# A three-layer graph network: another form of the last layer's sums, and gathers moved ahead of a layer's last rows

## The chip, the cores and the metric

The kernel runs on one core of a Trainium2 chip. The metric is device time in microseconds (us), lower is better. One launch computes the whole result; all inputs come from HBM and the output goes back there. A core has TensorE (PE in the profile; PEld is its weight load), VectorE (DVE), ScalarE (ACT), GpSimd (POOL) and SyncE (SP); each runs its own list of instructions in order, and waits on semaphores for the others. Indirect DMAs, which fetch or store rows whose numbers lie in a tile of indices, are issued by GpSimd. SP issues the plain ones.

## The reference

A graph of N = 6250 nodes and 100,000 edges (`src`, `dst`, sorted by `dst`), with 256 features for each node in float32. Three attention layers follow each other; the first two (GATv2, 4 heads of 64) also have an edge from each node to itself:

```python
xl = (x @ Wl).reshape(n, H, C); xr = (x @ Wr).reshape(n, H, C)
e = leaky_relu(xl[src] + xr[dst], 0.2)
logits = einsum('ehc,hc->eh', e, att)
alpha = softmax of logits over the edges that share a dst
out = segment_sum(xl[src] * alpha[:, :, None], dst) + b
...
x = layernorm(x + gat2(elu(gat1(x))))
...
Wh = einsum('nf,hfd->hnd', x, W)                        # 8 heads of 32
e = leaky_relu(s1[:, src] + s2[:, dst], 0.2)            # s1, s2: Wh times two vectors
out = segment_sum(softmax of e * Wh[:, src], dst)
x = layernorm(x + out)
```

So each layer fetches one row of a table for each edge, weighs it, and adds up the rows of each node.

## The kernel before

**The plan.** `make_plan` first sorts the nodes by falling degree into 49 blocks of 128 nodes, one node on each partition. Block b has a fixed number of columns `cols[b]`, the most edges that a node of it may have: 38, 25, 24, 23, 22, 21, 21, 20, ... down to 10, 10, 9, together 814. Column j of a block holds the j-th source of each of its 128 nodes; nodes with fewer edges point at a row `NP` that adds nothing. The plan leaves, for each block, the sources' numbers and the input rows (`near_d`), and writes the first table `xl1_d`, whose 261st element is the node's place in the sorted order. A flag `fits` says whether the degrees fit the columns; if not, `tile_general_path` computes everything in another way. With `fits` set, `tile_by_degree` runs.

**The three layers of `tile_by_degree`.** `layer2` runs twice (i = 0 and 1), then comes the third layer as a loop of its own. Each walks over the 49 blocks in order, and writes the next layer's table as it goes: layer 1 the rows of `xl2_d` and `xr2_d`, layer 2 those of `wh_d` (in the profile `whs_d`), layer 3 the output. Since any node can be a source, a layer's gathers read the whole table before them. The order is written out by hand, and the engines follow it.

For each column of a block `gather` issues one indirect DMA (128 rows of 260 to 264 floats) into row tiles of up to T = 9 columns; `chunks` cuts a block of up to 9, 18, 27 columns into 1, 2, 3 tiles, block 0 into 5. Layers 1 and 2 have 7 row tiles each, in pools of their own, layer 3 has 8. Block b + 1 is gathered ahead of the work on block b; how far GpSimd runs ahead is set by free row tiles.

In layers 1 and 2 VectorE computes, tile by tile, the maximum `z` (L1331, with weights prepared so that it gives the leaky ReLU), its product with `at` (L1332) and the sum over each head (L1333), in one of three `z` tiles. Then come the largest logit `top` (L1198), ScalarE's exponentials and their sums (L1205), the reciprocal (L1377), and the weighing of the rows (`weighted_sum`, L1235 on VectorE and L1234 on ScalarE); TensorE adds the rows up by multiplying each with the identity into `acc` (L1242). `end` of the block before and `finish` make the next table's row and send it with SP (L1430, L1431, L1463). At the start of layer 2 SP loads blocks 0 to 2 of both tables into `two` (L1439, L1440), later block b + 3.

In layer 3 TensorE does nothing. VectorE adds up the logits (L1496, L1500), finds the maximum (L1198), and after the exponentials weighs the rows in place (L1253). Then `added_up` sums the columns by halves: the second and third row tile are added to the first (L1262), then its upper half to its lower until two columns are left (L1265), and those two give `acc_v` (L1269). The rest is the normalisation (L1507, L1510, L1276, L1278, L1285) and an indirect DMA that scatters the block's rows to the output (`put_out`, L1525). The scatter of block b - 2 stands on GpSimd's queue behind the gathers of block b + 1.

After layer 1, `sources` (the numbers by which layer 1 gathers) are not needed; ScalarE has copied each row's 261st element into `spots` (L1343), by which layers 2 and 3 gather.

## Time and profile before

| | us |
|---|---|
| device time, median of 3 runs | 3926.89 |
| lowest and highest run | 3918.14, 3933.62 |
| device time of the profiled execution | 3945.85 |
| its span, first to last instruction | 3944.1 |
| first gather of layer 1, 2, 3 | 161.8, 1471.1, 2708.2 |
| last gather of layer 3 | 3905.5 |

The profiled execution is one of the longer ones: it lies 19 us above the median of the three runs. In the profile a group of instructions is named by its line, engine, operation and tiles, with its count, its busy time, the mean duration, and the time for which the engine stood idle just before it with what ended that. The mean granted clock of TensorE is 0.67 of full speed. The timeline has start, duration, engine, line and operation, and in brackets the idle time before it with its releaser ("issue" where nothing is seen that it waited for, "remote" where the releaser isn't known).

### The profile page before, as it was taken

The page shows a single profiled execution, that of the slowest core. Times are in us where ns is not written, and L with a number is a line of the kernel's source. Part 1 is how long each engine was busy: PE and PEld are TensorE (multiplying, and loading weights), DVE is VectorE, ACT ScalarE, POOL GpSimd, SP SyncE. Part 2 cuts the span into 40 slices and gives each one's busy share as a digit, 9 for nine tenths or more (in the row PEclk, how much of TensorE's full clock was granted, in tenths as well). Part 3 has the DMA queues.
Part 4 walks back from the last instruction along what each step waited for, and adds up shares of the span by engine and source line. Part 5 has one row for each costly group of instructions (what it writes and reads, how often), then busy time and mean ns, then how long its engine had stood idle before and what let it go on. Part 6 is the DMA issues. An engine that isn't in the chain of part 4 may idle for free.

```text
span 3944.1 us, 23710 instructions
## 1 busy us (share of the span) xinstructions
PE 1485.0 (38%) x5144; PEld 1107.1 (28%) x5145; DVE 2724.0 (69%) x2731; ACT 1102.9 (28%) x4179; POOL 2582.6 (65%) x2640
## 2 busy tenths in 40 slices
PE   5336556556676761455545455552000000000000
PEld 4224434344554541343433343442000000000000
DVE  6277778678788876888877888983655545444554
ACT  2124334334444441343434343541000000000000
POOL 6466666666666636666666666654777777776675
PEclk7667778777788886777666767776555555555555
DMA  8443333333343424343333343433333333333332
GB/s 185 103 96 99 98 100 105 100 98 102 104 107 103 106 74 101 98 111 107 106 107 107 106 112 104 118 104 58 102 100 97 102 99 100 99 97 84 82 99 72
DMA packets 197564, 399.63 MB, mean 101 GB/s; under 512 B 63516, under 2 KB 115994, under 8 KB 197396
## 3 DMA queue, kind: packets, MB, share of 16 engines
q0 software_dynamic: 123488, 342.06, 33.6%
q1 hardware_dynamic: 66226, 54.22, 4.8%
q10 hardware_dynamic: 7698, 1.74, 0.4%
q8 instruction: 45, 0.74, 0.1%
q14 instruction: 107, 0.88, 0.1%
HBM read 357.84 MB, written 40.42 MB: 101 GB/s over the span
## 4 chain that ended last, share of the span: by engine, by line
issue 23%; POOL 22%; DVE 15%; PE 13%; another core or an unknown queue 9%; ACT 6%; DMA 2%; DVEq 0%; ACTq 0%; POOLq 0%
POOL g L1485 15%; PE acc L1242 9%; POOL g L1311 5%; DVE z L1332 4%; DVE z L1331 4%; PE pm L1187 3%; ACT g L1234 3%; DVE lg L1333 2%; ACT wt L1205 2%; DVE g L1235 1%; DVE g L1253 1%; POOL out L1525 1%; ACT xT L1182 1%; DMA g<-whs_d,spots 1%
## 5 line engine op out<-in xcount | busy, mean ns | idle before, releaser
L1242 PE MATMUL acc<-g,ident 128*128 128x256 f32 x3452 | 1038.7, 462 | 940.8 <-issue 368.9
L1242 PEld LDWEIGHTS acc<-g,ident 128*128 128x128 f32 x3452 | 778.1, 233 | 1197.6 <-issue 618.4
L1311 POOL DMA_INDIRECT g<-xl_d,spots x814 | 772.5, 949 | 465.2 <-issue 227.5
L1311 POOL DMA_INDIRECT g<-xl_d,near_r x814 | 774.8, 952 | 427.8 <-issue 239.2
L1485 POOL DMA_INDIRECT g<-whs_d,spots x814 | 857.3, 1053 | 299.0 <-issue 292.6
L1234 ACT ACTIVATE g<-g,by 128x64 f32<-128x64 f32 x2064 | 560.2, 337 | 431.4 <-issue 429.4
L1331 DVE TENSOR_TENSOR z<-g,pr 128x1820 f32<-128x1820 f32 (+4 forms) x236 | 502.3, 2129 | 60.9 <-DMA g<-xl_d,spots 31.9
L1332 DVE TENSOR_TENSOR z<-z,at 128x1820 f32<-128x1820 f32 (+4 forms) x236 | 503.8, 2135 | 8.1
L1333 DVE TENSOR_REDUCE lg<-z 128x28 f32<-128x1820 f32 (+4 forms) x236 | 503.6, 2134 | 8.2
L1235 DVE TENSOR_TENSOR g<-g,wt 128x1792 f32<-128x1792 f32 (+5 forms) x236 | 354.0, 1518 | 2.9
L1215 ACT ACTIVATE wt<-lg 128x128 f32<-128x128 f32 (+17 forms) x49 | 14.0, 285 | 849.3 <-DVE lg L1214 245.2
L1496 DVE TENSOR_TENSOR lg<-g,s_r 128x56 f32<-128x56 f32 (+4 forms) x113 | 25.1, 223 | 314.3 <-DMA g<-whs_d,spots 281.8
L1253 DVE TENSOR_TENSOR g<-g,wt 128x1792 f32<-128x1792 f32 (+4 forms) x113 | 229.5, 2049 | 0.0
L1182 ACT COPY xT<-pt 128x256 f32<-128x256 f32 x147 | 55.0, 374 | 581.9 <-PE pt L1180 341.8
L1377 DVE RECIPROCAL den<-den 128x4 f32<-128x4 f32 x98 | 17.4, 178 | 240.6 <-ACT wt L1205 186.3
L1205 ACT ACTIVATE wt<-lg,top 128x19 f32<-128x19 f32 (+14 forms) x392 | 116.1, 296 | 219.9 <-DVE lg L1333 129.1
L1348 DVE TENSOR_TENSOR h<-acc,den 128x256 f32<-128x256 f32 x98 | 40.9, 417 | 158.6 <-remote 91.6
L1187 PE MATMUL pm<-wcat,xT 128*128 128x260 f32 x392 | 136.2, 506 | 35.9 <-ACT xT L1182 34.5
L1262 DVE TENSOR_TENSOR g<-g,g 128x1792 f32<-128x1792 f32 (+4 forms) x64 | 129.1, 2017 | 25.2 <-DVE g L1253 15.7
L1187 PE MATMUL pm<-wh_cat,xT 128*128 128x272 f32 x196 | 83.2, 564 | 128.9 <-ACT xT L1182 80.3
L1187 PEld LDWEIGHTS pm<-wcat,xT 128*128 128x128 f32 x392 | 95.5, 257 | 71.5 <-ACT xT L1182 50.9
L1525 POOL DMA_INDIRECT out<-y,node_i x49 | 51.4, 1049 | 70.0 <-ACT y L1288 54.4
(162 smaller groups left out, 1575.5 us busy)
## 6 DMA issues: line engine op xcount, KB each, us to landing
g<-xl_d,near_r POOLq DMA_INDIRECT x814
g<-xl_d,spots POOLq DMA_INDIRECT x814
g<-whs_d,spots POOLq DMA_INDIRECT x814
whs_d<-row SPq DMA_DIRECT2D x49, 132.0 KB
xl_d<-xl SPq DMA_DIRECT2D x49, 130.0 KB
xl_d<-row SPq DMA_DIRECT2D x49, 130.0 KB
xr_d<-row SPq DMA_DIRECT2D x49, 130.0 KB
two<-xl_d SPq DMA_DIRECT2D x49, 130.0 KB
```

The lines of the kernel that those rows point to most:

```text
L1187: nc.tensor.matmul(pm, xT[:, c, :], w[:, c, :], start=c == 0, stop=c == 1)
L1205: nc.scalar.activation(wt[:, :, h], lg[:, :S, h], AF.Exp, bias=top[:, h : h + 1], accum_out=den[:, h : h + 1],)
L1234: nc.scalar.mul(g4[:, t, h, :], g4[:, t, h, :], by[:, t - m, h : h + 1])
L1235: nc.vector.tensor_mul(g4[:, :m], g4[:, :m], wt[:, s0 : s0 + m, :].unsqueeze(3).to_broadcast([P, m, H, F // H]),)
L1242: nc.tensor.matmul(acc, ident, g4[:, t], start=s0 + t == 0, stop=s0 + t == S - 1)
L1253: nc.vector.tensor_mul(g4, g4, wt[:, s0:s1, :].unsqueeze(3).to_broadcast([P, n, H, width]))
L1262: nc.vector.tensor_add(t[:, :m], t[:, :m], u[:, :m])
L1311: nc.gpsimd.indirect_dma_start(out=g[:, s - s0, :], out_offset=None, in_=table, in_offset=source(of, b, s - 1),)
L1331: nc.vector.tensor_max(z, g[:, :n, :W2], xr[:, None, :].to_broadcast([P, n, W2]))
L1332: nc.vector.tensor_mul(z, z, at[:, None, :].to_broadcast([P, n, W2]))
L1333: nc.vector.reduce_sum(lg[:, s0:s1, :], z.rearrange("p t (h d) -> p t h d", h=H2), axis=AX.X)
L1485: nc.gpsimd.indirect_dma_start(out=g[:, s - s0, :], out_offset=None, in_=wh_d[:, :], in_offset=source(spots, b, s),)
```

## The change

It has four parts.

1. *Sums of layer 3.* The weighed rows go into a tile of their own, `prod` (up to 27 columns), in place of the row tile. One reduction then sums its columns, reading with a stride of 256 floats. Block 0, with 38 columns, takes two reductions and an addition.
2. *Gathers ahead of the last rows.* The sources of blocks 0, 1 and 2 are sorted by place during layer 1, by keys (place, column) with MAX8 and MATCH_REPLACE8, eight at a time. Of block 0 the first 14, of block 1 the first 12 and of block 2 the first 11 columns then name rows of blocks 0 to 44 alone, copied into `soon`. They are gathered from that part of the table before the last four blocks' rows are there: the calls stand behind the gathers of block 48 of the layer before, for layer 2 and for layer 3. SP's loads of `two` for blocks 0 to 2 move there too.
3. *Row tiles.* One pool of nine serves all three layers, with rows of 264 floats. To make room there is one `z` tile in place of three, `spots` lies in the memory of `sources`, and layer 3 has two `lg` tiles in place of three.
4. *A flag.* If any of the 37 columns names a later row, `done` stays 0. It is read at the end, and `tile_general_path` then computes everything; it is no longer the other branch of `fits`.

```diff
+EARLY = (14, 12, 11)
+LATE = 4
...
-    with tc.If(ok != 0) as branch:
+    with tc.If(ok != 0):
...
-    with branch.Else():
+    right = nc.values_load(done[0:1, 0:1], min_val=0, max_val=1)
+    with tc.If(right == 0):
         tile_general_path(
...
-    spots = consts.tile([P, NB, CM], I32, name="spots")
+    spots = sources
+    AHEAD = (NB - LATE) * P
+    KEY = CM.bit_length()
+    CK = -(-CM // 8) * 8
...
+    rowp = ctx.enter_context(tc.tile_pool(name="rows", bufs=9))
+    twop = ctx.enter_context(tc.tile_pool(name="two", bufs=3))
+    RW = max(W2 + 1, A1)
+    begun = {}
...
+    def gather_rows(b, rows, cut, own, table, of, width, j0, j1):
+        for g, (s0, s1) in zip(rows, cut):
+            for j in range(max(s0 - own, j0), min(s1 - own, j1)):
+                nc.gpsimd.indirect_dma_start(
+                    out=g[:, j + own - s0, :width], out_offset=None, in_=table,
+                    in_offset=source(of, b, j),
+                )
+
+    def row_tiles(b, own):
+        cut = chunks(cols[b] + own)
+        return [rowp.tile([P, T, RW], F32, name="g") for _ in cut], cut
+
+    def begin(own, table, width):
+        for b, n in enumerate(EARLY):
+            begun[b] = row_tiles(b, own)
+            gather_rows(b, *begun[b], own, table[:AHEAD], soon, width, 0, n)
+
+    def sort_sources(work, ps, b):
+        n = cols[b]
+        keys = work.tile([P, CK], F32, name="keys")
+        nc.vector.memset(keys, -float(NP << KEY))
+        nc.vector.tensor_single_scalar(
+            keys[:, :n], spots[:, b, :n], -float(1 << KEY), op=OP.mult
+        )
+        nc.vector.tensor_sub(keys, keys, number)
+        order = work.tile([P, CK], F32, name="order")
+        for r in range(0, CK, 8):
+            nc.vector.max(order[:, r : r + 8], keys)
+            if r + 8 < CK:
+                nc.vector.match_replace(keys, order[:, r : r + 8], keys, -BIG)
+        places = work.tile([P, CK], I32, name="places")
+        nc.vector.tensor_single_scalar(places, order, -1.0, op=OP.mult)
+        nc.vector.tensor_single_scalar(spots[:, b, :n], places[:, :n], KEY, op=OP.logical_shift_right)
+        e = EARLY[b]
+        nc.vector.tensor_single_scalar(soon[:, b, :e], spots[:, b, :e], AHEAD - 1, op=OP.min)
+        nc.vector.tensor_single_scalar(
+            late[:, b : b + 1], spots[:, b, e - 1 : e], float(AHEAD), op=OP.is_ge
+        )
+        if b + 1 == len(EARLY):
+            pb = ps.tile([P, b + 1], F32, name="pb", tag="tp")
+            nc.tensor.matmul(pb, ones, late, start=True, stop=True)
+            bad = work.tile([P, 1], F32, name="bad")
+            nc.vector.reduce_sum(bad, pb, axis=AX.X)
+            nc.vector.tensor_single_scalar(done, bad, 0.0, op=OP.is_equal)
...
-    def added_up(work, rows, cut, wts, H, width, between):
+    def added_up(work, prod, rows, cut, wts, H, width, between):
         wt, _ = wts
-        parts = []
-        for g, (s0, s1) in zip(rows, cut):
+        acc = work.tile([P, F], F32, name="acc_v", bufs=2)
+        base = 0
+        for k, (g, (s0, s1)) in enumerate(zip(rows, cut)):
             n = s1 - s0
-            g4 = g[:, :n, : H * width].rearrange("p t (h d) -> p t h d", h=H)
             nc.vector.tensor_mul(
-                g4, g4, wt[:, s0:s1, :].unsqueeze(3).to_broadcast([P, n, H, width])
+                prod[:, s0 - base : s1 - base, :].rearrange("p t (h d) -> p t h d", h=H),
+                g[:, :n, :F].rearrange("p t (h d) -> p t h d", h=H),
+                wt[:, s0:s1, :].unsqueeze(3).to_broadcast([P, n, H, width]),
             )
             if s0 == 0:
                 between()
-            parts.append((g[:, :, :F], n))
-        parts.sort(key=lambda part: -part[1])
-        t, n = parts[0]
-        for u, m in parts[1:]:
-            nc.vector.tensor_add(t[:, :m], t[:, :m], u[:, :m])
-        while n > 2:
-            m = n // 2
-            nc.vector.tensor_add(t[:, :m], t[:, :m], t[:, n - m : n])
-            n -= m
-        acc = work.tile([P, F], F32, name="acc_v")
-        if n == 2:
-            nc.vector.tensor_add(acc, t[:, 0], t[:, 1])
-        else:
-            nc.vector.tensor_copy(acc, t[:, 0])
+            if k + 1 == len(cut) or cut[k + 1][1] - base > prod.shape[1]:
+                part = acc if base == 0 else work.tile([P, F], F32, name="part_v", bufs=1)
+                nc.vector.reduce_sum(
+                    part, prod[:, : s1 - base, :].rearrange("p s f -> p f s"), axis=AX.X
+                )
+                if base:
+                    nc.vector.tensor_add(acc, acc, part)
+                base = s1
         return acc
...
-            rowp = es.enter_context(tc.tile_pool(name=f"rows{i}", bufs=7))
-            zp = es.enter_context(tc.tile_pool(name=f"z{i}", bufs=3))
+            zp = es.enter_context(tc.tile_pool(name=f"z{i}", bufs=1))
...
+                first = EARLY[b] if b in begun else 0
+                rows, cut = begun.pop(b) if first else row_tiles(b, 1)
+                gather_rows(b, rows, cut, 1, table, of, width, first, cols[b])
...
+                    if 0 < b <= len(EARLY):
+                        sort_sources(work, pst, b - 1)
...
                 if b + 1 < NB:
                     gather(b + 1)
+                if b + 2 == NB:
+                    follow()
...
+    def begin2():
+        begin(1, xl2_d, W2)
+        for b in range(3):
+            start2(b)
+            loaded.add((1, b))
+
+    layer2(0, xl1_d[:, :], sources, W2 + 1, start1, own1, finish1, begin2)
     last_weights()
-    layer2(1, xl2_d[:, :], spots, W2, start2, own2, finish2)
+    layer2(1, xl2_d[:, :], spots, W2, start2, own2, finish2, lambda: begin(0, wh_d, A1))
...
-        rowp = es.enter_context(tc.tile_pool(name="rows3", bufs=8))
...
-            lg = work.tile([P, CM, H1], F32, name="lg")
+            lg = work.tile([P, CM, H1], F32, name="lg", bufs=2)
...
+        prod = work.tile([P, 3 * T, F], F32, name="weighted", bufs=1)
```

## The prediction

> **What bounds the kernel now.** I read four views in this order: busy time by engine, the groups, the timeline of GpSimd at the two changes of layer, and the timeline of the last layer.
>
> ```profile
> PE 1485.0 (38%) x5144; PEld 1107.1 (28%) x5145; DVE 2724.0 (69%) x2731; ACT 1102.9 (28%) x4179; POOL 2582.6 (65%) x2640
> ...
> L1485 POOL DMA_INDIRECT g<-whs_d,spots x814 | 857.3, 1053 | 299.0 <-issue 292.6
> ...
> L1253 DVE TENSOR_TENSOR g<-g,wt 128x1792 f32<-128x1792 f32 (+4 forms) x113 | 229.5, 2049 | 0.0
> L1262 DVE TENSOR_TENSOR g<-g,g 128x1792 f32<-128x1792 f32 (+4 forms) x64 | 129.1, 2017 | 25.2 <-DVE g L1253 15.7
> ```
>
> No engine is full, so the bound changes by layer. The first gather of each layer starts at 161.8, 1471.1 and 2708.2 us, so the layers take 1309, 1237 and 1236 us. A gather costs 0.95 us and 0.30 us to the next one, a cadence of 1.25 us, and 814 of them are 1021 us in each layer.
>
> ```profile
> 1421.22 0.95 POOL L1311 DMA_INDIRECT g<-xl_d,near_r  x1 [0.30 <-issue]
> 1471.11 0.95 POOL L1311 DMA_INDIRECT g<-xl_d,spots  x1 [48.94 <-DMA xl_d<-row]
> ...
> 2658.97 0.94 POOL L1311 DMA_INDIRECT g<-xl_d,spots  x1 [0.30 <-issue]
> 2708.18 0.94 POOL L1485 DMA_INDIRECT g<-whs_d,spots  x1 [48.27 <-issue]
> ```
>
> At each change of layer GpSimd stands still for 48 us until the last row of the table has been written. In layers 1 and 2 it otherwise runs ahead: VectorE's waits for gathers are 22.1 us at the start of layer 1, 31.9 us at the start of layer 2, and none between. There VectorE and TensorE, with ScalarE between them, set the pace. In layer 3 it is the reverse: VectorE waits 281.8 us for gathers, and GpSimd's chain is the layer. Its 1198 us from 2708 to 3906 are 857 of gathers, 244 of gaps of 0.30, 62 for 46 scatters of the output, 30 of waits ahead of those, and little else. But its mean gather is 1053 ns here and 949 before:
>
> ```profile
> 3013.26 0.94 POOL L1485 DMA_INDIRECT g<-whs_d,spots  x1 [0.30 <-DVE g L1253]
> 3014.91 3.82 DVE L1262 TENSOR_TENSOR g<-g,g 128x1792 f32<-128x1792 f32 x2
> 3015.77 1.98 POOL L1485 DMA_INDIRECT g<-whs_d,spots  x1 [0.30 <-issue]
> 3018.05 1.49 POOL L1485 DMA_INDIRECT g<-whs_d,spots  x1 [0.30 <-issue]
> 3018.76 1.69 DVE L1265 TENSOR_TENSOR g<-g 128x768 f32<-128x768 f32 x2
> ```
>
> The reader sees gathers lengthen only while VectorE adds. Over the layer the excess above 949 ns is 84.5 us; put down to the VectorE instruction that overlaps each gather most, 62.5 falls on L1262, 13.3 on L1265, 0.7 on L1269, and 2.0 on the multiplication L1253, whose weights lie in PSUM.
>
> **What the Trainium skill says.** "SBUF — State Buffer", section "Who interferes with whom": an instruction with two SBUF inputs contends with a GpSimd instruction that reads SBUF, whereas `tensor_reduce` on trn2 "never contends". The first is what the lines above show; for the second, the reduces L1198 and L1218 together overlap 0.3 us of the excess, but they are short. The same page, section "Door 1: The DMA port swizzle", says that reads that go to a new 16-byte line with each access pay a penalty, without a figure. The trace has one: L1030, a sum over a stride of 49 floats, takes 2076 ns for 1078 elements, L1090 over neighbours 1022 ns for 834. With the 0.15 us that stand ahead of both, that is 1.79 and 1.04 ns an element. L1198 agrees: 323 ns at 96, 695 at 304 elements, 1.79 each.
>
> **The change, part by part,** against the profiled execution (span 3944.1, device time 3945.85).
>
> *Sums of layer 3.* Removed: L1262, L1265, L1269, 129.1 + 89.0 + 20.8 = 239 us of VectorE. Added: 50 reductions over 814 x 256 = 208,384 elements with a stride of 1 KB. At 1.04 ns they cost 225 us, at 1.79 they cost 381 us; I take 1.79, since the stride passes a line each time. VectorE is then busy 620 - 239 + 381 = 762 of some 1080 us in the layer, per block 0.27 S for the multiplication, 0.46 S for the sum and about 3.6 us for the rest, against 1.25 S + 1.3 on GpSimd. For the S of 9 to 25 columns GpSimd stays the longer. What it brings: the excess of 62.5 + 13.3 + 0.7 = 76.5 us. Multiplying into its own tile lets a row buffer go ahead of the sum, which costs nothing.
>
> *But GpSimd is not alone on the path throughout.* From block 14 to 35 and from 45 to 46 short dependent VectorE instructions each start 1 to 4 us late:
>
> ```profile
> 3272.87 0.30 DVE L1214 TENSOR_TENSOR lg<-lg,top 128x136 f32<-128x136 f32 x1 [1.00 <-issue]
> 3276.37 0.43 DVE L1510 TENSOR_TENSOR h<-h,near_r 128x256 f32<-128x256 f32 x1 [2.86 <-remote]
> 3277.77 0.43 DVE L1276 BATCH_NORM_STATS2 stats<-h 128x6 f32<-128x256 f32 x1 [0.97 <-DVE h L1510]
> ```
>
> A block then takes VectorE 25.2 us, whatever its columns; outside, block 37 took 11.4. GpSimd, up to 39 us ahead, waited 30 us ahead of scatters for it. The cause isn't in the trace. If those 22 blocks keep 25.2 us each (554 us), GpSimd's 351 gathers and 22 scatters need 470: 84 late, less 39 of lead, 45 of waits in place of 30, and the part brings 61. If it goes, the part brings 76.5 + 22 = 98. I take the middle, -80.
>
> *37 gathers early.* 37 x 1.25 = 46.4 us move into each 48 us standstill. They need the rows of blocks 0 to 44: block 44's writes are issued at 1419.5 and 2658.6, when GpSimd falls idle, so the early gathers end at about 1468 and 2707, just ahead of the last row's landing. They stand on GpSimd's queue behind the layer's last gather, so while they wait only later gathers wait behind them, which the missing rows hold up anyway. They want six row tiles, three are free at once, and three come free as blocks 46 and 47 are multiplied and summed, before their turn. In layer 3 all 46 us count, since GpSimd is the path: -46. In layer 2 VectorE is. Block 0 needs 24 more gathers after 1471, which end at 1501 where all 38 ended at 1519; its multiplication, at 1534.7, starts 18 to 21 us earlier, and with it TensorE's sum of block 0, which is next to be late:
>
> ```profile
> 1594.09 0.42 DVE L1348 TENSOR_TENSOR h<-acc,den 128x256 f32<-128x256 f32 x1 [24.83 <-remote]
> ```
>
> That wait keeps its length; all behind it shifts: -20. SP's six loads of `two` pass ahead of the last rows' writes and need only rows long written: nothing.
>
> *Sorting, on VectorE in layer 1.* 17 instructions for each of three blocks. MAX8 costs 978 ns for 784 elements, so 0.20 for 40; the replacement with its load about 0.28; the small ones 0.06 to 0.21: 3.5 us and 0.7 of gaps, 12.6 us for three. In block 2 it lies beside a wait of 7.3 us for TensorE; in blocks 1 and 3 about half is covered by ScalarE's exponentials: +6. The verdict on `late` waits for TensorE behind the sum that VectorE waits for anyway: nothing.
>
> *One z tile in place of three.* Each maximum now waits for the reduction of the tile before it. A dependent start comes 0.10 us later than a free one (1398.89 to 1400.59 against 1400.59 to 1402.39). 138 such pairs: 14 us at most, 0 if other waits cover it; +10.
>
> *Nine buffers in layers 1 and 2.* No gather is waited for there: 0; up to -10 at their starts. *The flag `done`*: one more load and branch on each engine at the very end, not shown after a layer; ScalarE's first instruction after the first such branch comes 0.6 us late. Between 1 and 8: +3. *Tail:* 37.6 us after the last gather, of which VectorE's late starts are some 20; the longer sums add 1.7 a block: -8 (-18 to +15).
>
> Sum: -80 - 46 - 20 + 6 + 10 + 3 - 8 = -135; span 3809, device time 3811. The runs' median lies 19 us under the profiled execution: 3792, so **3790 us**.
>
> **Rivals.**
> 1. *VectorE's late starts last as long as before or longer, and tail and transitions give less.* For: the period of 25.2 us did not depend on the columns, so shorter sums needn't shorten it. Against: it is 3 or 4 instructions a block fewer. -61 for the sums, +10 in the tail, -30 and -15 for the gathers: -77, median 3850.
> 2. *The late starts vanish with the adds*, since GpSimd no longer holds up VectorE, and GpSimd alone is the layer: -98, tail -18, rest as above: -163, and z and sorting hidden, -175: 3750. For: in blocks 0 to 12 and 36 to 43 there are none. Against: the first appeared in instructions that the change keeps.
> 3. *Slower: the strided sum lies on top of the late starts.* If the 25 us hold from block 18 to the end and the longer sum isn't hidden in them, a block takes 26 us; 31 blocks take 806 us where GpSimd needs 583. GpSimd finishes block 17 at 3160 (345 gathers and 16 scatters from 2708), the layer ends at 3966, with the tail of 11 and the rest -1 the span is 3976 and the median about 3957. It decides from about 26 such blocks; before there were 25 with a shorter sum, and they ended by themselves. A stride cost above some 4 ns an element would do the same.
> 4. *The flag is 0 and the general path runs as well*: milliseconds. A node would need over half of its 24 or more sources in 4 of 49 blocks. Under 1%.
>
> **How the numbers follow.** Forecast (3755 to 3825) 0.55, rival 1 0.25, rival 2 0.12, rival 3 0.08, rival 4 within it. The range 3735 to 3865 holds the first and nearly all of rivals 1 and 2 and leaves rival 3 out. A change under 0.5%, 20 us, can't be told from none. Faster 0.91, same 0.02, slower 0.07.
>
> **What would show it.** The mean gather in layer 3 near 955 ns; no gather over 1.5 us; 37 gathers of `whs_d` ahead of the last row's landing and a standstill of under 5 us; reductions of 4608 elements near 8.4 us (4.9 if the stride is free); layer 2 from its first late gather 20 us shorter. Wrong would be: VectorE's period above 25 us in most of layer 3, or gathers that still lengthen beside the reductions.

## The result and the profile after

| | us |
|---|---|
| kernel before, median of 20 runs (lowest, highest) | 3921.78 (3911.18, 3945.54) |
| changed kernel, median of 20 runs (lowest, highest) | 3910.64 (3903.90, 3930.62) |
| ratio, 95% interval | 0.9973 (0.9961 to 0.9984) |
| changed kernel's profiled execution: device time, span | 3906.24, 3904.4 |
| first late gather of layer 3, last gather (before: 2708.2, 3905.5) | 2729.3, 3855.0 |
| from the last gather to the end (before: 38.6) | 49.4 |

The change brought 11 us where 135 were forecast: a small gain, since the interval leaves 1 out. The two profiled executions stand 40 us apart, because that of the kernel before, at 3945.85, is longer than any of the 20 runs; so the experiments below are compared by the ratios of their runs, each to the kernel before on the same chip in the same group. On six of seven occasions the kernel before took 3922 to 3943 us, and in the third group of experiments, on a chip that no other group of experiments used and that is called the other chip here, 3532 us.

GpSimd's groups in the changed kernel (count, busy time, mean ns of one, idle time before them):

```profile
L1207 POOL DMA_INDIRECT g<-whs_d,near_r x777 | 802.2, 1032 | 293.9 <-issue 251.9 <-DVE lg L1567 29.4 <-DVE weighted L1327 8.4
...
L1207 POOL DMA_INDIRECT g<-whs_d,soon x37 | 35.0, 946 | 28.5 <-DVE mv L1348 17.5 <-issue 10.7 <-PE acc L1316 0.3
```

And VectorE's:

```profile
L1336 DVE TENSOR_REDUCE acc_v<-weighted 128x256 f32<-128x4096 f32 (+16 forms) x49 | 349.2, 7127 | 11.7 <-remote 6.1 <-issue 2.3 <-DVE weighted L1327 2.0
...
L1415 DVE TENSOR_TENSOR h<-acc,den 128x256 f32<-128x256 f32 x98 | 40.7, 416 | 166.8 <-remote 122.3 <-PE acc L1316 44.4
L1567 DVE TENSOR_TENSOR lg<-g,s_r 128x56 f32<-128x56 f32 (+4 forms) x113 | 22.8, 214 | 367.4 <-DMA g<-whs_d,near_r 300.0 <-issue 31.8 <-DMA out<-y,node_i 29.0
```

The 37 early gathers are there and the strided sums cost a little less than forecast (349 us in place of 381), yet the mean gather of layer 3 is 1032 ns, hardly less than the 1053 of the kernel before. The timeline of layer 3 shows that gathers beside a sum can keep their length, and lengthen with none beside them. First a sum of 20 columns beside the gathers of block 8, then a place 424 us later:

```profile
2948.65 8.71 DVE L1336 TENSOR_REDUCE acc_v<-weighted 128x256 f32<-128x5120 f32 x1
2949.35 0.94 POOL L1207 DMA_INDIRECT g<-whs_d,near_r  x1 [0.30 <-issue]
2950.60 0.96 POOL L1207 DMA_INDIRECT g<-whs_d,near_r  x1 [0.31 <-issue]
2951.86 0.95 POOL L1207 DMA_INDIRECT g<-whs_d,near_r  x1 [0.30 <-issue]
...
3372.67 0.21 DVE L1567 TENSOR_TENSOR lg<-g,s_r 128x64 f32<-128x64 f32 x1
3372.84 1.14 POOL L1207 DMA_INDIRECT g<-whs_d,near_r  x1 [0.30 <-issue]
3374.28 1.79 POOL L1207 DMA_INDIRECT g<-whs_d,near_r  x1 [0.30 <-issue]
3376.38 1.10 POOL L1207 DMA_INDIRECT g<-whs_d,near_r  x1 [0.30 <-issue]
```

Up to 3004 us, 69 gathers lie wholly beside a strided sum: mean 0.947 us, longest 0.98. From block 10 on, 570 gathers have a mean of 1.062 us, and the long ones come in sizes (139 near 1.09, 33 near 1.24, 33 between 1.5 and 1.94 us) also while VectorE and ScalarE do nothing. That is 65 us, and 41 gaps of up to 1.6 us in place of 0.30 add 21: GpSimd is held up for 86 us, in a manner that is rare in the kernel before, where nearly all of the excess lies beside the adds. VectorE's own late starts, other than the waits for gathers, went from some 185 pieces and 270 us (2800 to 3890 us of the kernel before) to 27 pieces and 39 us (2800 to 3850 us).

Two more places show what may be the same thing. At the end, small VectorE instructions that need only one another start late:

```profile
3859.79 0.24 DVE L1571 SCALAR_TENSOR_TENSOR lg<-lg 128x80 f32<-128x80 f32 x1 [0.24 <-DVE lg L1567]
3861.19 0.29 DVE L1272 TENSOR_REDUCE top<-lg 128x8 f32<-128x80 f32 x1 [1.16 <-DVE lg L1571]
3861.89 0.24 DVE L1288 TENSOR_TENSOR lg<-lg,top 128x80 f32<-128x80 f32 x1 [0.41 <-DVE top L1272]
...
3863.99 0.42 DVE L1581 TENSOR_TENSOR h<-h,near_r 128x256 f32<-128x256 f32 x1 [1.52 <-DVE h L1578]
3865.39 0.43 DVE L1346 BATCH_NORM_STATS2 stats<-h 128x6 f32<-128x256 f32 x1 [0.98 <-DVE h L1581]
```

Their starts are whole multiples of 0.70 us apart (1.40, 0.70, 2.10, 1.40). And at the end of layer 2:

```profile
2687.96 0.63 PE L1254 MATMUL pt<-ident,near_r 128*128 128x128 f32 x2
...
2698.91 0.95 POOL L1207 DMA_INDIRECT g<-whs_d,soon  x1 [0.30 <-issue]
2705.92 0.42 DVE L1415 TENSOR_TENSOR h<-acc,den 128x256 f32<-128x256 f32 x1 [25.33 <-remote]
2705.96 0.37 ACT L1256 COPY xT<-pt 128x256 f32<-128x256 f32 x1 [27.81 <-remote]
```

TensorE's transposes are recorded as done at 2688.6. VectorE and ScalarE, which wait for TensorE alone, go on at 2705.9, that is 17 us later and 7.0 us after the start of the last early gather. So the last rows were sent off at 2726 us, and a standstill of 29.4 us was left. In the kernel before ScalarE goes on 0.04 us after the same transposes:

```profile
2698.62 0.38 PE L1180 MATMUL pt<-ident,near_r 128*128 128x128 f32 x2
...
2699.04 0.37 ACT L1182 COPY xT<-pt 128x256 f32<-128x256 f32 x1 [7.25 <-PE pt L1180]
```

The trace also keeps the moments at which semaphores are raised, which these views don't print, and they tell which link is late. TensorE's increments, due by 2688.6, are recorded at 2691.11, 2696.01, 2704.42 and 2705.81, then 0.04 to 0.05 us apart up to 2705.94, and ScalarE starts 0.02 us after the last. By this record it isn't that an engine notices a result late: the increment itself comes late. And the record of increments is thin: it holds 8,814 by DMAs, where 2,919 DMAs raise 16 each (the traces of the third group show it), 46,704 in all. From 2800 to 3800 us it has 282 to 286 increments of any kind in each 200 us, which is one in 0.70 us, the step on which the small instructions start. Waits that the lines put down to "remote" or "issue" may be such increments that the trace has lost.

### The profile page after: what moved, and what is told of

It reads as the page before. It is cut to its first block, busy times and chain, and to the rows that moved or that the text cites. A ratio compares the mean times of both kernels' runs of the same rounds, so it can differ in the third digit from the quotient of the medians.

```text
span 3904.4 us, 23669 instructions
## 1 busy us (share of the span) xinstructions
PE 1465.1 (38%) x5147; PEld 1100.0 (28%) x5147; DVE 2859.7 (73%) x2624; ACT 1093.2 (28%) x4179; POOL 2558.8 (66%) x2642
## 4 chain that ended last, share of the span: by engine, by line
issue 24%; POOL 21%; PE 16%; DVE 14%; another core or an unknown queue 12%; ACT 9%; DMA 2%; DVEq 0%; SPq 0%; ACTq 0%; POOLq 0%
POOL g L1207 19%; PE acc L1316 10%; ACT g L1308 4%; PE pm L1261 3%; DVE z L1397 3%; DVE z L1396 3%; DVE lg L1398 3%; ACT wt L1279 2%; DVE weighted L1327 1%; DVE g L1309 1%; DMA g<-xl_d,near_r 1%; POOL out L1597 1%; ACT xT L1256 1%; PE pl L1261 1%
## 5 line engine op out<-in xcount | busy, mean ns | idle before, releaser
L1207 POOL DMA_INDIRECT g<-xl_d,near_r x1591 | 1508.6, 948 | 843.6 <-issue 455.7
L1316 PE MATMUL acc<-g,ident 128*128 128x256 f32 x3452 | 1015.0, 455 | 910.1 <-issue 361.4
L1316 PEld LDWEIGHTS acc<-g,ident 128*128 128x128 f32 x3452 | 768.0, 229 | 1152.9 <-issue 617.4
L1207 POOL DMA_INDIRECT g<-whs_d,near_r x777 | 802.2, 1032 | 293.9 <-issue 251.9
L1308 ACT ACTIVATE g<-g,by 128x64 f32<-128x64 f32 x2064 | 550.4, 337 | 331.3 <-issue 328.0
L1397 DVE TENSOR_TENSOR z<-z,at 128x1820 f32<-128x1820 f32 (+4 forms) x236 | 503.7, 2134 | 8.1
L1336 DVE TENSOR_REDUCE acc_v<-weighted 128x256 f32<-128x4096 f32 (+16 forms) x49 | 349.2, 7127 | 11.7 <-remote 6.1
L1327 DVE TENSOR_TENSOR weighted<-g,wt 128x1792 f32<-128x1792 f32 (+4 forms) x113 | 229.5, 2048 | 0.0
L1415 DVE TENSOR_TENSOR h<-acc,den 128x256 f32<-128x256 f32 x98 | 40.7, 416 | 166.8 <-remote 122.3
L1261 PEld LDWEIGHTS pm<-wh_cat,xT 128*128 128x128 f32 x196 | 46.0, 260 | 213.5 <-issue 113.5
```

The source lines that it names most:

```text
L1207: nc.gpsimd.indirect_dma_start(out=g[:, j + own - s0, :width], out_offset=None, in_=table, in_offset=source(of, b, j),)
L1261: nc.tensor.matmul(pm, xT[:, c, :], w[:, c, :], start=c == 0, stop=c == 1)
L1308: nc.scalar.mul(g4[:, t, h, :], g4[:, t, h, :], by[:, t - m, h : h + 1])
L1316: nc.tensor.matmul(acc, ident, g4[:, t], start=s0 + t == 0, stop=s0 + t == S - 1)
L1327: nc.vector.tensor_mul(prod[:, s0 - base : s1 - base, :].rearrange("p t (h d) -> p t h d", h=H), g[:, :n, :F].rearrange("p t (h d) -> p t ...
L1336: nc.vector.reduce_sum(part, prod[:, : s1 - base, :].rearrange("p s f -> p f s"), axis=AX.X)
```

## The experiments

Each set of runs shares a chip with its own runs of the kernel before. Ratios have their 95% intervals. Three theories are tested: A, that the sums no longer lengthen gathers, but that a new hold-up sets in once VectorE waits for gathers; its rival B, that the sums gave what was forecast and the rest was lost in layers 1 and 2. C came after the first group: gathers issued back to back hold up results of TensorE.

### First group: one part at a time (the kernel before: 3938.75 us)

The new sums in the kernel before:

```diff
-    def added_up(work, rows, cut, wts, H, width, between):
+    def added_up(work, prod, rows, cut, wts, H, width, between):
...
-            acc = added_up(work, rows, cut, wt, H1, D1, between)
+            acc = added_up(work, prod, rows, cut, wt, H1, D1, between)
```

> The kernel before with the new sums alone: products into a tile of their own, one strided TENSOR_REDUCE in place of the halving adds; no sorting, no early gathers, three z tiles, seven and eight row buffers. Theory A (a new hold-up): beside the strided sum a gather keeps its 0.95 us, but once VectorE has caught up and waits for gathers in every block, gathers are held up in another way (1.09, 1.24 and 1.79 us, and 0.9 us ahead of some). Then layer 3's gathers have a mean near 1.03 us here too, and the kernel is only 15 to 30 us below the kernel before (ratio 0.992 to 0.996). Theory B (the sums gave what was forecast, the missing part was lost in layers 1 and 2): mean gather 0.955 us, 80 us below the kernel before (ratio 0.980).

Measured: ratio 0.9969 (0.9952 to 0.9986), 12 us. Layer 3's gathers have a mean of 1040 ns, the longest 2.04 us, though the kernel has none of the rest of the change. The hold-up starts in block 7, at about 2930 us. So the sums alone gave little, and it was not a loss in layers 1 and 2 that took their gain.

The halving adds in the changed kernel:

```diff
-    def added_up(work, prod, rows, cut, wts, H, width, between):
+    def added_up(work, rows, cut, wts, H, width, between):
...
-            acc = added_up(work, prod, rows, cut, wt, H1, D1, between)
+            acc = added_up(work, rows, cut, wt, H1, D1, between)
```

> The changed kernel with the halving adds of the kernel before in layer 3; sorting, early gathers, one z tile and nine buffers kept. Theory A: the early gathers save 46 us in layer 3 and lose about 20 at the layers' ends, so 15 to 30 us slower than the changed kernel, about level with the kernel before (3915 to 3940), with gathers of 2 to 3 us beside the first halving add and few of 1.09 to 1.24 us. Theory B: 80 us slower than the changed kernel, near 3990.

Measured: 1.0042 (1.0030 to 1.0054). The changed kernel came to 0.9960 to 0.9973 on four occasions, so the old sums cost about 29 us there. That fits theory A. With e1_sums_only the sums are worth 12 to 29 us, not 80.

No early gathers, no sorting:

```diff
+    nc.vector.memset(done, 1)
...
         for b, n in enumerate(EARLY):
-            begun[b] = row_tiles(b, own)
-            gather_rows(b, *begun[b], own, table[:AHEAD], soon, width, 0, n)
+            pass
...
-                    if 0 < b <= len(EARLY):
-                        sort_sources(work, pst, b - 1)
```

> The changed kernel without the early gathers and without the sorting of three blocks' sources (all columns gathered when their layer's rows are all written; the flag is set at once); strided sums, one z tile and nine buffers kept. If running gathers beside a layer's last blocks is what makes those blocks end later, layer 2's first gather comes at 1471 to 1480 us (1418 early and 1495 late in the changed kernel) and layer 3's at 2708 to 2715 (2729 late), with the last gather 46 us minus 15 to 21 us later: 25 to 30 us slower than the changed kernel, 3935 to 3940. If the later ends come from the single z tile or the sorting's place, layer 2 starts after 1485 and layer 3 after 2720: 3945 to 3960.

Measured: 1.0048 (1.0035 to 1.0061), so the early gathers with their sorting are worth about 31 us in all. But layer 3's first gather came at 2725.6 us, and in e1_sums_only, on the same chip, at 2701.9: without early gathers, the changed kernel's layers 1 and 2 end 24 us later. That is near the second reading, which named the z tile or the sorting's place; the sorting isn't in this kernel, and which other part does it is left open.

Layer 3's sums on TensorE, which has nothing to do there:

```diff
-            acc = added_up(work, prod, rows, cut, wt, H1, D1, between)
+            acc = weighted_sum(ps, rows, cut, wt, H1, D1, between)
```

> The changed kernel with layer 3's sums made by TensorE, which is idle there (an identity matmul per gathered column into PSUM, as in layers 1 and 2); VectorE multiplies in place and does no sum. All else kept. If the new hold-up of gathers comes from VectorE waiting for gathers, whatever it does besides, it stays or grows: mean gather 1.03 us or more and 3890 to 3915. If it comes from the strided sum, or from TensorE standing idle, gathers return to 0.95 to 0.96 us and cadence to 1.25: layer 3 is 777 x 1.25 + 49 x 1.3 = 1035 us from first late to last gather instead of 1126, and the kernel ends near 3815.

Measured: 1.0261 (1.0248 to 1.0275), 4039 us. Gathers have a mean of 951 ns, as the second reading said, yet the kernel is far slower, which neither foresaw. Its timeline shows why:

```profile
3319.49 9.70 PE L1316 MATMUL acc<-g,ident 128*128 128x256 f32 x36 [4.55 <-issue]
...
3349.06 0.95 POOL L1207 DMA_INDIRECT g<-whs_d,near_r  x1 [0.31 <-issue]
3355.97 0.42 DVE L1578 TENSOR_TENSOR h<-acc,den 128x256 f32<-128x256 f32 x1 [32.67 <-remote]
```

The matmuls are over at 3329.2. VectorE's `h`, which waits for TensorE and nothing else, starts at 3355.97, 6.9 us after GpSimd has started its last gather before a pause: the pattern of the end of layer 2. Its increments are late here too: three between 3331 and 3348, and a burst from 3355.69 to 3355.95. Over the layer `h` waits 837 us. In both places TensorE's results come late while gathers are issued back to back.

The traces so far also sort out what the hold-up of gathers goes with. Taking the gathers over 1.04 us that no add overlaps, their excess over 0.949 us is 64 us in the changed kernel and 73 in e1_sums_only, but 6 in the kernel before, 3 in e2_old_sums and 1 in e4_pe_sums. So where results arrive late it comes with the strided sums, and TensorE's idleness doesn't explain it, since TensorE is idle in the kernel before and in e2_old_sums too. Whether the sum itself sets it off, or the closer run of gathers that it allows, isn't shown.

### Second group: what costs layers 1 and 2, and what holds the gathers up (before: 3924.74 us)

One z tile in e1_sums_only:

```diff
-            zp = es.enter_context(tc.tile_pool(name=f"z{i}", bufs=3))
+            zp = es.enter_context(tc.tile_pool(name=f"z{i}", bufs=1))
```

> The kernel before with the strided sums (as in e1_sums_only) and with one z tile in place of three; row buffers, gathers and all else as in the kernel before. The changed kernel without early gathers (e3_no_early) reached layer 3's first gather 24 us later than e1_sums_only, with one z tile and nine row buffers as the main differences. If the single z tile costs it: first gather of layer 3 at 2720 to 2728 us and about 24 us slower than e1_sums_only (ratio to the kernel before 1.002 to 1.005). If the nine buffers or the other layout of rows and lists cost it: first gather near 2702 to 2710 and ratio 0.996 to 0.999.

Measured: 0.9965 (0.9954 to 0.9977), as with three tiles. A cost of one z tile is not seen.

Useless sums on VectorE in layer 3:

```diff
+        S = cut[-1][1]
+        more = min(round(1.2 * S - 3.6), S)
+        if S < 20 and more > 0:
+            again = work.tile([P, F], F32, name="part_v", bufs=1)
+            nc.vector.reduce_sum(
+                again, prod[:, :more, :].rearrange("p s f -> p f s"), axis=AX.X
+            )
         return acc
```

> The changed kernel with useless extra work on VectorE in layer 3: after each block's strided sum a second strided sum over 7 to 19 of its columns (for blocks of under 20 columns), about 0.435 us per column, so that VectorE is busy nearly all the time and hardly waits for gathers. It adds 3 to 8 us of VectorE time to 39 blocks, 230 us in all, and changes no result. Theory A (gathers are held up because VectorE waits for them): the 1.09, 1.24 and 1.79 us gathers from block 10 on become few, mean gather 0.96 to 0.98 us instead of 1.03, last gather 30 to 80 us sooner, and the kernel with more work is 20 to 70 us faster than the changed kernel (3840 to 3890). Rival (something else holds the gathers up from some 280 us into layer 3 on, or the strided sum does): mean gather stays 1.03 us or more, and the kernel is level with the changed kernel or up to 60 us slower.

Measured: 1.0020 (1.0007 to 1.0033), some 20 us slower than the changed kernel. GpSimd's gathers and, from VectorE's groups, the extra sums and the waits for gathers:

```profile
L1207 POOL DMA_INDIRECT g<-whs_d,near_r x777 | 803.4, 1034 | 288.6 <-issue 245.0 <-DVE lg L1574 30.1 <-DVE weighted L1327 8.3
```

```profile
L1346 DVE TENSOR_REDUCE part_v<-weighted 128x256 f32<-128x4096 f32 (+10 forms) x39 | 243.2, 6237 | 0.0
...
L1574 DVE TENSOR_TENSOR lg<-g,s_r 128x56 f32<-128x56 f32 (+4 forms) x113 | 21.7, 210 | 144.1 <-DMA g<-whs_d,near_r 104.2 <-issue 28.9 <-DMA whs_d<-row 6.6
```

VectorE's waits for gathers fell from 300 to 104 us, and the gathers stayed at 1034 ns, held up from block 10 on, as in the changed kernel. In the changed kernel VectorE waits 5 to 10 us in each of blocks 5 to 9, and hardly a gather is held up there. So theory A, as far as it says that VectorE's waiting sets the hold-up off, fell. The filler left some waits, so it isn't excluded that they keep it up.

Early gathers in layer 2 alone:

```diff
-    layer2(1, xl2_d[:, :], spots, W2, start2, own2, finish2, lambda: begin(0, wh_d, A1))
+    layer2(1, xl2_d[:, :], spots, W2, start2, own2, finish2, lambda: None)
```

> The changed kernel with the early gathers of layer 2 alone; layer 3 gathers all 814 columns after its rows are written. In the changed kernel, 37 early gathers run back to back from 2654 to 2700 us, and from 2681 on VectorE and ScalarE wait 25 and 28 us for a result of TensorE that its records show done 17 us before they go on, at 2706, 7 us after the last early gather. Theory C (gathers issued back to back hold up the signal): without them this wait is gone, layer 2's rows are all written 15 to 25 us sooner, near 2705, and the whole costs 46 minus about 20: 22 to 30 us slower than the changed kernel. Rival (the wait is there anyway): rows written near 2727, 46 us slower than the changed kernel.

Measured: 1.0018 (1.0007 to 1.0029), so layer 3's early gathers are worth 20 us of their 46. The long wait at the end of layer 2 is gone. The last ScalarE copy of layer 2's results starts at 2714.3 us, and in e6_filler, whose layers 1 and 2 are those of the changed kernel, on the same chip at 2745.0. So running 37 gathers beside the last blocks put these off by 31 us.

Two z tiles in the changed kernel:

```diff
-            zp = es.enter_context(tc.tile_pool(name=f"z{i}", bufs=1))
+            zp = es.enter_context(tc.tile_pool(name=f"z{i}", bufs=2))
...
-    ones = consts.tile([P, P], F32, name="ones_l")
+    ones = consts.tile([P, 1], F32, name="ones_l")
```

> The changed kernel with two z tiles in place of one (the sort's scratch tiles and the flag's column made smaller to make room for it). If the single z tile costs 20 us or more in layers 1 and 2, this is 10 to 24 us faster than the changed kernel (3887 to 3900); if nine buffers or the layout cost it, no change within 5 us.

Measured: 0.9962 (0.9945 to 0.9978), the changed kernel's own ratio. It agrees with e5_one_z.

### Third group: the other chip (before: 3532.10 us)

Seven row buffers in e3_no_early:

```diff
-    rowp = ctx.enter_context(tc.tile_pool(name="rows", bufs=9))
+    rowp = ctx.enter_context(tc.tile_pool(name="rows", bufs=7))
```

> The changed kernel without early gathers and sorting (as e3_no_early), with seven shared row buffers in place of nine. e3_no_early reached layer 3's first gather 24 us later than the kernel before with strided sums, and the single z tile is no cause of it (e5_one_z: ratio 0.9965 with one, 0.9969 with three). If the nine buffers cost it (GpSimd runs further ahead in layers 1 and 2): layer 3's first gather 20 us or more sooner than in e3_no_early, ratio to the kernel before 0.997 to 1.000. If another part does (lists inside near_r, wider rows, rows two loaded ahead): first gather as late as in e3_no_early, ratio 1.003 to 1.007.

Layer 3's early gathers in three groups, each behind a step of VectorE:

```diff
+    tick = consts.tile([P, 2], F32, name="tick")
+    tock = consts.tile([P, 2], F32, name="tock")
...
+    def begin3(b, n):
+        if b:
+            nc.vector.memset(tick[:, b - 1 : b], 0.0)
+            nc.gpsimd.tensor_copy(tock[:, b - 1 : b], tick[:, b - 1 : b])
+        begun[b] = row_tiles(b, 0)
+        gather_rows(b, *begun[b], 0, wh_d[:AHEAD], soon, A1, 0, n)
...
                     rest = end(b - 1, acc, den)
+                if i == 1 and b + 2 >= NB:
+                    begin3(b + 3 - NB, EARLY[b + 3 - NB])
...
-    layer2(1, xl2_d[:, :], spots, W2, start2, own2, finish2, lambda: begin(0, wh_d, A1))
+    layer2(1, xl2_d[:, :], spots, W2, start2, own2, finish2, lambda: begin3(0, EARLY[0]))
```

> The changed kernel with layer 3's early gathers in three groups of 14, 12 and 11 in place of 37 back to back: before the second and the third group GpSimd waits until VectorE has divided the sums of the third last and of the second last block of layer 2. Theory C (gathers issued back to back for more than some 20 us hold up the results of TensorE; when GpSimd stops, they arrive 7 us later): the wait of 25 us at the end of layer 2 shrinks to under 10, layer 2's rows are written 10 to 17 us sooner, and the kernel is 8 to 17 us faster than the changed kernel (ratio to the kernel before 0.993 to 0.995). Rival (the early gathers hold the last blocks up through what they move, not through being issued without a break): no gain, ratio 0.996 to 0.998.

Useless matmuls beside layer 3:

```diff
+        idle = ps.tile([P, F], F32, name="idle", bufs=1)
+        for _ in range(1900):
+            nc.tensor.matmul(idle, ident, wh[:, 0, :F], start=True, stop=True)
         gather(0)
```

> The changed kernel with 1,900 useless matmuls in layer 3, which TensorE runs one after another beside the rest, waiting for nothing and waited for by nothing. In layer 3 from about 280 us on, gathers take 1.09, 1.24 and 1.79 us and small instructions start late in steps of 0.70 us. If this comes from TensorE standing idle (the one engine that has nothing to do there): gathers return to a mean of 0.95 to 0.97 us, and the kernel is 60 to 85 us faster (3825 to 3850). If not: no change within 10 us, mean gather 1.03 us.

Seven row buffers and 26 early gathers:

```diff
-EARLY = (14, 12, 11)
+EARLY = (14, 12)
...
-    rowp = ctx.enter_context(tc.tile_pool(name="rows", bufs=9))
+    rowp = ctx.enter_context(tc.tile_pool(name="rows", bufs=7))
```

> The changed kernel with seven row buffers in place of nine, and 26 early gathers (of two blocks) in place of 37. If nine buffers cost 24 us in layers 1 and 2: 24 us sooner less 11 gathers of 1.25 us in layers 2 and 3 as far as they counted, so 5 to 15 us faster than the changed kernel (ratio to the kernel before 0.993 to 0.996). If they cost nothing: 5 to 15 us slower than the changed kernel (ratio 0.998 to 1.001).

| | ratio | us less than before |
|---|---|---|
| e9_seven_rows: sums, one z tile, seven buffers, no early gathers | 0.9817 (0.9804 to 0.9831) | 64 |
| e10_paused: the whole change, early gathers in three groups | 0.9661 (0.9648 to 0.9675) | 120 |
| e11_pe_busy: the whole change, useless matmuls | 0.9664 (0.9651 to 0.9677) | 120 |
| e12_seven_26: the sums, 26 early gathers, seven buffers | 0.9696 (0.9683 to 0.9709) | 109 |

The questions these runs were made for are left open by them, since the signs they were to remove are in none of the four profiles. GpSimd's and VectorE's groups in e11_pe_busy:

```profile
L1207 POOL DMA_INDIRECT g<-whs_d,near_r x777 | 738.3, 950 | 244.6 <-issue 230.6 <-DVE weighted L1327 8.8 <-DMA out<-y,node_i 2.4
```

```profile
L1415 DVE TENSOR_TENSOR h<-acc,den 128x256 f32<-128x256 f32 x98 | 40.6, 414 | 9.6 <-PE acc L1316 9.6
```

Gathers take 950 ns, and `h` waits 9.6 us for TensorE where it waited 166.8. The useless matmuls are not the cause: e9_seven_rows has none of them, and its 814 gathers take 949 ns. Neither has a small late start of VectorE in layer 3. The end of layer 2, with the same 37 gathers issued back to back beside it:

```profile
2318.77 0.95 POOL L1207 DMA_INDIRECT g<-whs_d,soon  x1 [0.30 <-issue]
2318.94 0.38 PE L1254 MATMUL pt<-ident,near_r 128*128 128x128 f32 x2
2319.36 0.37 ACT L1256 COPY xT<-pt 128x256 f32<-128x256 f32 x1 [3.55 <-PE pt L1254]
```

ScalarE goes on 0.04 us after the transposes, in the middle of the gathers. On VectorE and GpSimd the durations are the same on both chips (a median gather of layer 3 is 946 ns here and 946 to 950 there, and the 236 multiplications of z by the attention vector take 503.7 us in both); what differs is how late one engine's result, or its own, reaches the next instruction. The record of semaphores differs with it: the four traces from this chip hold 46,732 to 46,742 increments by DMAs, 16 for each of the 2,919 and a few more; the sixteen others hold 7,851 to 9,133, under a fifth.

### Further groups: the same kernels again (before: 3943.41, 3938.51, 3940.14 us)

The changed kernel itself (three times), the kernel before itself, e1_sums_only and e9_seven_rows were repeated without an edit, to see the change itself on the other chip. All of them ran where the kernel before takes 3938 to 3943 us.

> The changed kernel itself, as it is. If this chip is one on which results of TensorE arrive late and gathers are held up (the kernel before near 3920 to 3940 us): ratio 0.996 to 0.999, gathers in layer 3 1.03 us in the mean. If it is one without these signs (the kernel before near 3530 us) and the chip took the gain away: ratio 0.963 to 0.969, gathers 0.95 us, the 37 early gathers of layer 3 worth 40 us or more. If the gain of the last group came from its additions (pauses, useless matmuls, seven buffers) and not from the chip: ratio 0.990 or more on such a chip too.

> The kernel before itself, for its profile on the same chip. On a chip without the signs: no late starts in steps of 0.70 us, gathers in layer 3 lengthened only beside the halving adds (2 to 3 us each beside the first add), 75 to 110 us in all; standstills of GpSimd of 45 to 50 us at the layers' ends. On a chip with them: a profile like the first one of the kernel before, within 30 us.

> The kernel before with the strided sums alone (the kernel of e1_sums_only). On a chip without the signs, if the sums are worth what was forecast: 65 to 95 us less than the kernel before (ratio 0.973 to 0.982 of 3532), and the early gathers bring the rest of the way to 0.966. On a chip with the signs: 0.996 to 0.998 as before.

> The changed kernel itself once more. On a chip without the signs (the kernel before near 3530 us): ratio 0.963 to 0.969 and gathers of 0.95 us in layer 3 if the chip took the gain away; 0.990 or more if the additions of the third group made it. On a chip with the signs (3920 to 3945 us): 0.996 to 0.999, which decides nothing more.

> The changed kernel itself. On a chip without late results (the kernel before near 3530 us): ratio 0.963 to 0.969 if the chip took the gain away, 0.990 or more if the additions of the third group made it. On a chip with them: 0.995 to 0.999.

> The kernel of e9_seven_rows (no early gathers, seven row buffers in place of nine). On a chip with late results: first gather of layer 3 20 us or more sooner than in e3_no_early, ratio to the kernel before 0.996 to 0.999, if nine buffers cost the 24 us; first gather as late as there and ratio 1.003 to 1.007 if the other layout of rows and lists costs them. On a chip without: 0.982 again.

| | ratio |
|---|---|
| e13_after_again | 0.9968 (0.9957 to 0.9980) |
| e14_before_again | 1.0001 (0.9993 to 1.0010) |
| e15_sums_again | 0.9975 (0.9961 to 0.9988) |
| e16_after_third | 0.9960 (0.9948 to 0.9972) |
| e17_after_fourth | 0.9962 (0.9943 to 0.9982) |
| e18_seven_again | 0.9975 (0.9959 to 0.9991) |

The result repeats. In e13_after_again the wait at the end of layer 2 is 21.4 us, and in e16_after_third 25.5, so it belongs to the place and not to one execution; in e14_before_again it is 5.8, and VectorE has some 185 late starts in layer 3, as in the first profile. And e18_seven_again answers what e9_seven_rows could not: with seven row buffers the ratio is 0.9975 where e3_no_early with nine has 1.0048. That is 29 us, though the medians of the two groups make it 18. The first gathers of layer 3 in e3_no_early and in e18_seven_again:

```profile
2725.56 0.94 POOL L1208 DMA_INDIRECT g<-whs_d,near_r  x1 [63.52 <-PEq L700]
...
2710.85 0.94 POOL L1208 DMA_INDIRECT g<-whs_d,near_r  x1 [49.19 <-PEq L700]
```

The ratio is as expected; the first gather comes 15 us sooner, and not 20, in single executions on two chips. So the nine buffers cost layers 1 and 2 between 15 and 29 us where results arrive late. Why they do isn't shown. On the other chip no cost is seen: the last ScalarE copy of layer 2 starts at 2339.4 us in e11_pe_busy with nine and at 2338.6 in e12_seven_26 with seven.

## Why the prediction was wrong

| step | forecast, us | where results arrive late (about 3940) | on the other chip (3532) |
|---|---|---|---|
| sums of layer 3, with the tail | -80 - 8 | -12 (e1; -10 by e15, -29 by e2) | with the next line -64 (e9) |
| one z tile | +10 | 0 (e5, e8) | |
| early gathers of layer 3 | -46 | -20 (e7) | with the next line -56 (e9 to e11) |
| early gathers of layer 2, sorting | -20 + 6 | -12 (e3 to e7) | |
| nine buffers in layers 1 and 2 | 0 to -10 | +15 to +29 (e3, e18) | none seen (e11, e12) |
| flag `done` | +3 | within the others | within the others |
| the whole change, as measured | -135 | -11 to -16 | -120, with additions (e10, e11) |

**Sums of layer 3: the step that failed.** The working was that gathers are lengthened only by the adds, 76.5 us, and that without them a gather takes 0.95 us. The first half holds: beside the strided sums gathers take 0.947 us, which is what the Trainium skill says in "SBUF — State Buffer", section "Who interferes with whom", of `tensor_reduce` on trn2, and the adds' 2 to 3 us are gone. The second half does not: 86 us of another hold-up took their place, from block 10 on, and the sums alone brought 12 us. It is a hold-up that the kernels without strided sums hardly have. The prediction had what may be its sign before it, VectorE's late starts in blocks 14 to 35, and treated them as VectorE's affair: either they last (rival 1, 3850) or they vanish (rival 2, 3750). What it did not allow for is that VectorE's late starts shrink to 39 us and GpSimd, which sets the end, is then held up itself. On the other chip, where nobody is held up, the gathers of the layer are at their cadence: in e11_pe_busy 1040.6 us from first late to last gather, where 777 x 1.25 + 49 x 1.3 is 1035. Of the signs that it named, the 37 gathers ahead of the last landing came; the mean gather of 955 ns, no gather over 1.5 us (there were 33) and a standstill under 5 us did not.

**Early gathers of layer 3.** Their 46 us were counted in full since "GpSimd is the path". They end at 2699.9, and the step that they would finish "just ahead of the last row's landing" took that landing at its old time: the last rows were sent off at 2705 before. Running beside layer 2's last blocks the gathers put this off to 2726, and that was not thought of at all. On chips with late results 20 of 46 us are left. On the other one the early and late gathers follow within 1.8 us (2341.3 and 2343.1 in e11_pe_busy).

**Early gathers of layer 2** brought 12 with the sorting, near the 14 forecast, but this is luck: two larger terms nearly cancel. From layer 1's first gather to layer 2's first late one e3_no_early takes 1321 us, and e2_old_sums and e4_pe_sums, with early gathers on the same chip, 1352: these put off the end of layer 1, like that of layer 2, by 31 us. From there to layer 3's first gather e7_early2_only takes 1205 us, where e3_no_early takes 1246: a gain of 41, not 20. "That wait keeps its length" was right: the wait of `h` for block 0 was 24.83 us before and is 27.02 after.

**Nine buffers** were taken as no gain or a small one, with the reason that no gather is waited for there. A cost was not bounded, and with 15 to 29 us it is an error as large as that of layer 3's early gathers. **One z tile** was taken at 10, and 0, the lower bound given, was right; that other waits cover it is likely, but not shown.

**Tail.** -8 with bounds -18 to +15; it grew by 11 us, within the bounds, and late starts are seen in it. On the other chip it is 25.5 us.

**Strided sums** were priced at 1.79 ns an element and measured 1.70 (8.71 us for 5120, start included), so the stride costs about what the prediction took.

On the chip without late results the kernels that hold the whole change stand at 0.966, and the forecast was 3790 / 3926.89 = 0.965. So its accounting of gathers, sums and standstills comes near that chip; that the two ratios agree so closely is in part luck, as the forecast was worked out from a profile with 390 us more in it. That the change itself without additions does the same there was not measured: e11_pe_busy and e10_paused are the nearest, and there is no profile of the kernel before from that chip. What stays open is what makes results late. It goes with the chip or the occasion, since the same kernel has and hasn't got it; on such occasions it goes with gathers issued back to back (e4, e7), each of which raises 16 semaphore increments; whether pauses in the gathers help there wasn't settled, as e10_paused ran on the other chip. One rival was not tested: that the recording itself holds increments up. For it speaks that they are late in just the sixteen traces that lose most of them, and on the step at which they enter the record. All executions on record carry the profiler's span and clock, and none was taken without it, so the 390 us may belong in part to the measuring. A version that clearly beats the changed kernel was not found; one with seven buffers and early gathers was not run where nine of them cost.

## What to carry to other kernels

A wait whose releaser is long done, and small dependent instructions that start on a common step, suggest that something outside the kernel's own work sets times: work that is removed there need not come off the end, and the engine that is on the path may inherit the delay. Before such a profile is used as an account, it is worth counting the semaphore increments that it keeps against those that the program makes, and having one of the same kernel from another chip. Work moved into a standstill is worth its length only if what the standstill waits for isn't put off by it: check who else is running in that stretch.

## What the runs showed of the hardware that was not expected

- The same kernel takes 3532 us on one chip and 3922 to 3943 us on other occasions. VectorE's durations and a median gather are equal (503.7 us for the 236 multiplications, 946 to 950 ns) and the granted clocks of TensorE near each other (0.69 in e9_seven_rows, 0.67 in the changed kernel); the difference is in waits.
- On those other occasions TensorE's increments of its semaphore came up to 17 us (end of layer 2) and 27 us (e4_pe_sums) after its recorded end, the last of them about 7 us after GpSimd's last gather of a run; small VectorE instructions started at steps of 0.70 us, and in layer 3 one increment in 0.70 us entered the record; gathers took 1.09, 1.24 and 1.79 us with no instruction of another engine beside them (near 3374 us of the changed kernel).
- Summing over a stride of 1 KB costs VectorE 1.70 ns an element and leaves GpSimd's gathers at 0.947 us. TensorE, otherwise idle in layer 3, works through the sum of a block of 18 columns, 36 records, in 9.7 us; yet with the sums there the kernel took 2.6% longer than the one before, as the results came late.
